# Layer 0's node table in rows of 268 values, x read from the input: a two-layer graph attention kernel

## The chip, the cores and the metric

The kernel runs on one core of a Trainium2 chip. The metric is the device time of one execution in microseconds, the median of several runs. The core has five engines that run their own instruction streams and signal each other: TensorE (PE), VectorE (DVE), ScalarE (ACT), GpSimd (POOL) and SyncE (SP); 16 DMA engines move data between DRAM and the on-chip memory (SBUF).

## The reference

A graph of N = 6250 nodes with 256 features each and E = 200000 edges, sorted by destination, with 32 attributes each. Two layers of graph attention with 4 heads and then 1:

```python
def _gat(x, src, dst, ea, Wg, a_s, a_d, Wge, a_e, b, n, h, f):
    hx = (x @ Wg).reshape(n, h, f)
    he = (ea @ Wge).reshape(-1, h, f)
    al = leaky_relu(einsum('nhf,hf->nh', hx, a_s)[src] + einsum('nhf,hf->nh', hx, a_d)[dst]
                    + einsum('ehf,hf->eh', he, a_e), 0.2)
    m = segment_max(al, dst, num_segments=n)
    al = exp(al - m[dst])
    al = al / segment_sum(al, dst, num_segments=n)[dst]
    out = segment_sum(hx[src] * al[:, :, None], dst, num_segments=n)
    return out.reshape(n, h * f) + b

h = maximum(layernorm(x), 0)
# in each layer: te = relu(edge_attr @ We + be) * exp(h @ Wo + bo)[src]; a loop edge per node
# with the mean te of its edges; layer 0: h1 = relu(_gat(h, ...) + h); layer 1: h2 = _gat(h1, ...) + h1
# result: x + h2 + h
```

## The kernel before, in words

**Tables.** For each layer there is a table in DRAM, `T[l]`, with one row per node. The useful part of a row of layer 0 has `TW` = 268 float32 values: the 256 projected features, 4 logit parts of the source, the gate exp(h Wo + bo), a one, 4 logit parts of the destination, and the two numbers (scale and offset) of the layer norm. A row of layer 1 has 260. Each row is stored twice as wide: its second half holds the node's own features, x for layer 0, the layer's input for layer 1. So the table is read in two ways: as N rows of 2 TW values, when the nodes of a step are loaded with their x, and as 2N rows of TW values, when rows are gathered by source (`self.rows`). The source indices `self.src` (128 partitions, one column per chunk of 128 edges) are therefore doubled.

**The start** (`prologue`, L203) makes the layer-0 table. The nodes are cut into 49 tiles of 128, in nine groups of 2, 5, 7, 7, 7, 7, 7, 5 and 2; after them come 24 tiles whose rows of x are gathered directly (`first_rows`, L252) for the first step's edges. A loop over the tiles writes out by hand which part of which tile comes next on each engine: statistics (DVE), `norm` (ACT, L318), `turn` (two transposes on PE, L324, copied by ACT, L326), `mult` (PE, L452), `keep` (DVE adds the bias into one of three `trow` buffers, L456), and for each group `store` (L339), which sends its rows to the table by an SP DMA (L343). `keep_x` (L346) copies a group's x into the second halves from the input `xt`, DRAM to DRAM, by an SP DMA (L350); one is issued every fourth tile from tile 8 on. `xt` is x padded with zeros to 268 values a row. Among the tiles, one piece at a time, `indices` (L458) prepares the index tables on DVE: it loads `sc0`, `bcol`, `drow`, `r4`, `src` and `dpv` by SP DMAs in this order, doubles `src` in four DVE operations (L478), and then works on the others (L481 and on).

**The steps** (`edges`, L649). Each layer is 66 steps of up to 24 chunks of 128 edges; a step covers the edges of at most 112 destination nodes. The pieces of a step are interleaved by the order of calls in the loop. Around the change:

- `nodes` (L905) issues one SP DMA for a step two ahead: 112 rows `tw` (the row and x) at a row number that SP loads into a register.
- `gather` (L839) issues the 24 indirect DMAs of the next step on POOL (L846): each fetches 128 rows by 128 indices of `src`. Three buffers `G` take turns.
- `logits` makes the edge logits on DVE, closing with two scans (L1058, L1060). `ends` (L1064) then has PE transpose their last columns (L1067).
- `spread` (L952, DVE L964 and L965, the wide operation L964 once for two steps), `parts` (DVE L993 to L996, PE L1001), `rphase1` and `rphase2` (the edge features on PE and ACT) belong to the next step; `links` (DVE L1077, L1079, PE L1084), `maxima` and `scale` (DVE L1148, 6.3 us) to this one.
- `sums` (PE L1160) adds the scaled rows by destination, 48 matmuls into one bank `u`; `evict` (ACT L1165) copies it to `U`. `finish`, one step later, makes the nodes' result; in layer 0 `rows3` stores it to `T[1]` by an SP DMA (L1294).

`ending` (L744) does the last two steps of a layer. A second program for other graphs (`general`, L1307) is built but not run with these inputs.

Of the kernel before, what the change touches and what calls it, by code (L numbers as in the profile page):

```python
# [22 lines left out]
F32 = mybir.dt.float32  # L23
BF = mybir.dt.bfloat16
I32 = mybir.dt.int32
AF = mybir.ActivationFunctionType
OP = mybir.AluOpType
# [4 lines left out]
P = 128  # L32
C = 24
SE = P * C
NX = 24
D = 256
# [3 lines left out]
M = 112  # L40
# [39 lines left out]
class Kernel:  # L80
# [10 lines left out]
    def run(self):  # L91
        nc, tc = self.nc, self.tc
        self.cp = self.pool("consts")
        self.dp = self.pool("tables", space=DRAM)
        N = self.N
        self.T = [self.dp.tile([N + P, L.TW * 2], F32, name=f"T{L.l}") for L in self.L]

        self.rows = [t[0:N + P, :].rearrange("n (k w) -> (n k) w", w=L.TW) for t, L in zip(self.T, self.L)]
        with ExitStack() as c:
            c.enter_context(tc.manual_schedule())  # L100
            self.gp = [self.pool("gath0", 1, c)]
            self.ps_k = self.pool("ps_k", 1, c, space=PSUM)
            self.lp = self.pool("loads", 2, c)
            self.offs = offs = np.concatenate([[0], np.cumsum(self.cs)]).tolist()
            self.steps = [dict(L=L, s=s, C=self.cs[s], o=offs[s], k=L.l * self.NS + s)
                          for L in self.L for s in range(self.NS)]
            self.prologue()
            self.edges(c)
        self.general()
# [93 lines left out]
    def prologue(self):  # L203
        nc, tc, cp, a, N = self.nc, self.tc, self.cp, self.a, self.N
        L = self.L[0]
        H = L.H
        NT = -(-N // P)
        GT = 7
        CX = self.CX = min(self.cs[0], NX)
        V = nc.vector  # L210
        with ExitStack() as c:
            xp = self.pool("x", 1, c)
            wp = self.pool("pw", 2, c)
            pt = self.pool("pt", 2, c, space=PSUM)
            starts = sorted({*range(0, NT, GT), min(2, NT), max(NT - 2, 0)} - {NT})
            groups = [list(range(g, e)) for g, e in zip(starts, starts[1:] + [NT]) if g < e]
            g0 = len(groups)
# [25 lines left out]
            zero = wp.tile([P, 2 * L.TW], F32, name="zero", bufs=1)  # L243
            nc.gpsimd.memset(zero, 0.0)
            if NT * P < N + P:
                nc.sync.dma_start(self.T[0][NT * P:N + P, :], zero[:N + P - NT * P, :2 * L.TW])
            trows = [wp.tile([P, GT, L.TW], F32, name=f"trow{i}", bufs=1) for i in range(3)]
            ln = wp.tile([P, NT + CX, 2], F32, name="ln", bufs=1)

# [89 lines left out]
            def store(g):  # L339
                n, ts, trow = len(groups[g]), groups[g], trows[g % 3]  # L340
                nc.scalar.activation(trow[:, :n, L.ln:L.ln + 2], ln[:, ts[0]:ts[0] + n, :], AF.Copy)
                nc.scalar.activation(trow[:, :n, L.g:L.g + 1], trow[:, :n, L.g:L.g + 1], AF.Exp)
                nc.sync.dma_start(self.T[0][0:NT * P, :].rearrange("(p t) d -> p t d", p=P)  # L343
                                  [:, ts[0]:ts[0] + n, 0:L.TW], trow[:, :n, :])

            def keep_x(g):  # L346
                ts, n = groups[g], len(groups[g])
                to, of = (t.rearrange("(p t) d -> p t d", p=P)[:, ts[0]:ts[0] + n, :]
                          for t in (self.T[0][0:NT * P, L.TW:2 * L.TW], a["xt"][0:NT * P, :]))
                nc.sync.dma_start(to, of)  # L350

            lead = stats(0)
            for _ in range(6):
# [17 lines left out]
            for k in range(-3, len(tiles) + 1):  # L371
                if k == 6:
                    next(index)
                    gi = self.index_load(0, wp)
                    index = chain(index, self.index_group(0, wp, gi))
                if k > 10 and k % 2 or k > NT:
                    next(index, None)
                n0 = next(tail, None) if k >= NT // 2 else None
                if n0 is not None:
                    w = min(P, N + P - n0)  # L380
                    nc.sync.dma_start(self.T[1][n0:n0 + w, :], zero[:w, :2 * self.L[1].TW])
                if k == 5:
                    more()
                if k >= 8 and k % 4 == 0 and k // 4 - 2 < g0:
                    keep_x(k // 4 - 2)
                if 0 <= k + 1 < len(tiles):
                    turn(*tiles[k + 1])
                if 0 <= k + 3 < len(tiles):
                    g, i, t = tiles[k + 3]
                    if i == 0:  # L390
                        load(g + 3)
                        drain(ahead.pop(g, ()))
                    norm(g, i, t)
                step(g + 2)
                if t >= NT:
                    step(g + 2)
                if 0 <= k - 1 < len(tiles):
                    keep(*tiles[k - 1])
                step(g + 2)
                if t >= NT:  # L400
                    step(g + 2)
                if 0 <= k < 10 or k >= 14 and k % 4 == 0:
                    next(rows0, None)
                if k >= NT + 2:
                    next(later, None)
                if k == max(NT - 6, 7):
                    while not hasattr(self, "flags"):
                        next(index)
                    next(index)
                    self.load_lb(0)  # L410
                    self.load_ea(0)
                    self.load_fl(0)
                if 0 <= k < len(tiles):
                    mult(*tiles[k])
                while kept < g0 and groups[kept][-1] <= k - (3 if k < NT - 3 else 1):
                    store(kept)
                    kept += 1
# [40 lines left out]
    def indices(self, wp):  # L458


        nc, cp, a = self.nc, self.cp, self.a
        NS, NCH, N = self.NS, self.NCH, self.N
        V = nc.vector
# [9 lines left out]
        dpv = wp.tile([P, NS], I32, name="dpv", bufs=1)  # L473
        nc.sync.dma_start(dpv, a["dpv"])
        yield
        for i in range(0, NCH, 392):
            src = self.src[:, i:min(NCH, i + 392)]
            V.tensor_scalar(src, src, 2.0, None, op0=OP.mult)  # L478
            yield
        scf = wp.tile([P, 11, NS], F32, name="scf", bufs=1)  # L480
        V.tensor_copy(scf, sc0)  # L481
        V.memset(scf[:, 0, 0:1], 0.0)
# [20 lines left out]
        for r in range(2):  # L503
            n = (NS + 1 - r) // 2
# [334 lines left out]
    def gather(self, st):  # L839
        nc, L = self.nc, st["L"]  # L840
        st["G"] = G = self.G0 if st["k"] == 0 else self.gp[st["k"] % 3].tile([P, C, 270], F32, name="G")
        n = self.N
        idx = self.src[:, st["o"]:st["o"] + st["C"]]
        last = st["C"] - 1
        for c in (range(0) if st["k"] == 0 and self.CX > last else (last, *range(last))):
            nc.gpsimd.indirect_dma_start(  # L846
                out=G[:, c, 0:L.TW], out_offset=None, in_=self.rows[L.l][0:2 * n, :],
                in_offset=bass.IndirectOffsetOnAxis(ap=idx[:, c:c + 1], axis=0))

    def pair(self, k):  # L850
# [54 lines left out]
    def nodes(self, st):  # L905
        nc, L, s = self.nc, st["L"], st["s"]
        st["r"] = r = self.row(0, s)
        tw = self.tws[st["k"] % 4]
        st["tw"], st["xw"] = tw[:, :L.TW], tw[:, L.TW:L.TW + D]
        w = L.TW + D  # L910
        nc.sync.dma_start(tw[1:M + 1, :w], self.T[L.l][ds(r, M), 0:w])

    def halves(self, st):

# [147 lines left out]
        yield  # L1062

    def ends(self, st):  # L1064

        e = st["ends"]
        self.nc.tensor.transpose(self.lf[0:e.shape[1], 1:P + 1], e, self.ident)  # L1067
# [255 lines left out]
    def general_layer(self, L, wp, pp):  # L1323
        nc, tc, N, a = self.nc, self.tc, self.N, self.a
        V = nc.vector
        l, H = L.l, L.H
# [10 lines left out]
        with tc.For_i(0, self.NCH * P, P) as i:  # L1337
            si = wp.tile([P, 1], I32, name="gsi")
            di = wp.tile([P, 1], I32, name="gdi")
# [7 lines left out]
            G = wp.tile([P, 272], F32, name="gG")  # L1347
            nd = wp.tile([P, L.TW], F32, name=f"gnd{l}")
            old = wp.tile([P, L.W], F32, name=f"gold{l}")
            sw, dw = [wp.tile([P, 1], I32, name=n) for n in ("gsi2", "gdi2")]  # L1350
            V.tensor_scalar(sw, si, 2.0, None, op0=OP.mult)
            V.tensor_scalar(dw, di, 2.0, None, op0=OP.mult)
            for t, tab, ix in ((G[:, :L.TW], self.rows[l], sw), (nd, self.rows[l], dw), (old, state, di)):
                nc.gpsimd.indirect_dma_start(out=t, out_offset=None, in_=tab[:, :],
                                             in_offset=bass.IndirectOffsetOnAxis(ap=ix[:, 0:1], axis=0))
# [19 lines left out]
            t = wp.tile([P, P], F32, name="gt")  # L1375
# [11 lines left out]
            for v, f in ((G, G[:, L.p:L.p + H]), (old, e[:, 1, :H])):  # L1387
# [8 lines left out]
                                         out_offset=bass.IndirectOffsetOnAxis(ap=di[:, 0:1], axis=0))  # L1396
# [26 lines left out]
def drain(g):  # L1423
    for _ in g:
        pass
# [22 lines left out]
def layout(inputs):  # L1448
    x = np.ascontiguousarray(inputs["x"])
    src, dst, ea = (np.asarray(inputs[k]) for k in ("src", "dst", "edge_attr_32"))  # L1450
    N, E = x.shape[0], src.shape[0]
    cs = cuts(E)
    NS, NCH = len(cs), sum(cs)
    a = {"x": np.concatenate([x, np.zeros((2 * P, D), np.float32)])}
    a["xt"] = np.concatenate([a["x"], np.zeros((N + 2 * P, Layer(0).TW - D), np.float32)], 1)
    EP = NCH * P
    gdst = np.full(EP, N, np.int32)
    gdst[:E] = dst
# [13 lines left out]
    o = 0  # L1472
# [22 lines left out]
    for l, H in enumerate(HEADS):  # L1495
        w = {n: np.asarray(inputs[f"L0_gnn_{n}{l}"]) for n in _W}
# [23 lines left out]
```

## Time and profile before

| | us |
|---|---|
| median of 3 runs | 4721.76 |
| lowest, highest | 4721.40, 4724.88 |
| the profiled execution | 4717.79 |
| its span in the profile | 4716.0 |

| engine | busy us | share of the span |
|---|---|---|
| PE | 3204.3 | 68% |
| DVE | 2842.0 | 60% |
| ACT | 524.2 | 11% |
| POOL | 3015.5 | 64% |

The mean granted clock of PE is 0.73. The first gather from the layer-0 table starts at 105.6 us, the steps of layer 0 fill the time up to some 2370 us, those of layer 1 the rest. A line of the timeline gives start, duration, engine, line of the kernel, operation, result `<-` operands, the count of instructions taken together, and in brackets how long the engine stood before it and what it stood for. "SPq" is a DMA issued by SyncE, "PEld" TensorE's loading of weights. A line of the groups gives the same for all instructions of one kind: busy time and mean in ns, then the idle time before them, with what ended most of it. A line of the waits gives who waited `<-` for whom: total us, times, longest us.

### The profile page before, as it was taken

The numbers are of one execution on the slowest core, as the hardware profiler recorded it, in microseconds if no ns is written. First come the engines' busy times: TensorE is split into PE (matmuls) and PEld (weight loads), VectorE is DVE, ScalarE is ACT, GpSimd is POOL, SyncE is SP. The second block draws the span as 40 slices with busy tenths as digits, with TensorE's granted clock in tenths as the row PEclk, the third lists the DMA queues.
The fourth block names the chain that finished last, engine by engine and source line by source line (L and its number), as shares of the span: only waits on it lengthen the run. The fifth ranks groups of instructions, "written<-read, shape, count | busy, mean of one in ns | idle before, by whom it ended". The sixth has DMA issues, their size and how long they took to land. (4 is left out here: it accounts for less than half of the span.)

```text
span 4716.0 us, 33666 instructions
## 1 busy us (share of the span) xinstructions
PE 3204.3 (68%) x9878; PEld 1931.3 (41%) x9878; DVE 2842.0 (60%) x6122; ACT 524.2 (11%) x1162; POOL 3015.5 (64%) x3255
## 2 busy tenths in 40 slices
PE   7677677776777777777755666666666666666666
PEld 5344444444444444444433334343433333343434
DVE  6566676666676666666664555555545555554546
ACT  4111111111111111111110000000000000000000
POOL 5566666666666666666636666666666666666664
PEclk8767767767777777676676777776777777776777
DMA  8344444444444444444434444444444444444442
GB/s 275 94 128 128 117 126 131 119 127 128 116 127 129 125 122 126 127 121 126 122 84 113 120 118 127 116 123 121 124 117 122 127 121 119 119 125 114 122 124 74
DMA packets 234171, 582.99 MB, mean 124 GB/s; under 512 B 62185, under 2 KB 84613, under 8 KB 233913
## 3 DMA queue, kind: packets, MB, share of 16 engines
q0 software_dynamic: 150144, 422.75, 34.1%
q1 hardware_dynamic: 83419, 157.36, 10.1%
q8 instruction: 79, 1.29, 0.1%
q14 instruction: 113, 0.93, 0.1%
q10 hardware_dynamic: 416, 0.67, 0.1%
HBM read 549.44 MB, written 37.92 MB: 125 GB/s over the span
## 5 line engine op out<-in xcount | busy, mean ns | idle before, releaser
L846 POOL DMA_INDIRECT G<-T,src x3102 | 2962.0, 955 | 1623.1 <-issue 898.9
L1160 PE MATMUL u<-G,S 128*128 128x270 f32 (+1 forms) x6252 | 1621.4, 411 | 750.2 <-issue 628.7
L1160 PEld LDWEIGHTS u<-G,S 128*128 128x128 f32 x6252 | 1235.8, 200 | 1075.8 <-issue 682.0
L935 PE MATMUL y<-ea,webd 64*128 64x384 f32 (+1 forms) x1056 | 734.8, 822 | 304.5 <-issue 269.2
L1148 DVE TENSOR_TENSOR G<-G,kps 128x6144 f32<-128x6144 f32 (+3 forms) x136 | 853.0, 6275 | 0.0
L1077 DVE TENSOR_TENSOR_SCAN cl<-fl,cl,lf 4x129 f32<-4x129 f32 (+1 forms) x130 | 61.2, 471 | 937.2 <-remote 657.0
L935 PEld LDWEIGHTS y<-ea,webd 64*128 64x128 f32 x1056 | 290.2, 298 | 597.1 <-issue 534.7
L949 PE MATMUL zad<-R,wea 128*64 128x384 f32 (+1 forms) x1056 | 464.3, 794 | 2.3 <-ACT R L940 1.0
L980 DVE TENSOR_TENSOR S<-kps,loc 128x3072 f32<-128x3072 f32 x132 | 437.6, 3315 | 4.5
L940 ACT ACTIVATE R<-y,webd 128x768 f32<-128x768 f32 x260 | 233.1, 897 | 627.6 <-PE y L935 272.3
L949 PEld LDWEIGHTS zad<-R,wea 128*64 128x64 f32 x1056 | 155.9, 202 | 314.1 <-issue 253.5
L1165 ACT ACTIVATE U<-u 128x270 f32<-128x270 f32 (+1 forms) x132 | 51.9, 393 | 1880.4 <-remote 913.1
L1029 DVE STREAM_TRANSPOSE rt<-zad 128x768 f32<-128x768 f32 (+1 forms) x130 | 124.5, 958 | 35.2 <-remote 27.8
L1067 PE MATMUL lf<-ident,fb 128*36 128x128 f32 (+1 forms) x132 | 47.1, 357 | 138.2 <-issue 108.7
L1001 PE MATMUL zad<-a,Q 128*128 128x12 bf16 (+1 forms) x132 | 24.4, 185 | 156.6 <-issue 98.5
L452 PE MATMUL fin<-wg,h1T 128*128 128x260 f32 x264 | 127.2, 632 | 1.8 <-ACT h1T L1255 1.8
L1094 DVE TENSOR_TENSOR fb<-flpen,lf 128x192 f32<-128x192 bf16 (+1 forms) x132 | 36.7, 278 | 148.2 <-PE lf L1084 128.6
L964 DVE TENSOR_TENSOR lb<-lb,kps 128x1536 bf16<-128x1536 bf16 (+1 forms) x68 | 113.0, 1661 | 0.0
L452 PE MATMUL ps<-wg,hT 128*128 128x266 f32 x292 | 89.9, 436 | 33.3 <-ACT hT L326 14.9
L452 PEld LDWEIGHTS fin<-wg,h1T 128*128 128x128 f32 x264 | 71.5, 299 | 48.5 <-issue 34.6
L1001 PEld LDWEIGHTS <-Q 128*128 128x128 bf16 x132 | 14.9, 113 | 180.2 <-issue 104.4
L1190 ACT ACTIVATE mw<-mw,mg 128x2 f32<-128x2 f32 x66 | 19.7, 298 | 608.0 <-DVE mg L1189 337.1
(191 smaller groups left out, 2079.4 us busy)
## 6 DMA issues: line engine op xcount, KB each, us to landing
G<-T,src POOLq DMA_INDIRECT x3102
ea<-in_ea_dram SPq DMA_DIRECT2D x64, 768.0 KB
lb<-locrow SPq DMA_DIRECT2D x64, 384.0 KB
tw<-T SPq DMA_DIRECT2D x66, 229.2 KB
T<-t1row SPq DMA_DIRECT2D x66, 227.5 KB
tw<-T SPq DMA_DIRECT2D x66, 225.8 KB
out_dram<-fb SPq DMA_DIRECT2D x64, 112.0 KB
T<-in_xt_dram SPq DMA_DIRECT2D x5, 938.0 KB
```

What stands on the lines that cost most here:

```text
L452: self.nc.tensor.matmul(ps[:, :L.MW], hT[:, k, :], self.wg[L.l][:, k, :], start=(k == 0), stop=(k == 1))
L846: nc.gpsimd.indirect_dma_start(out=G[:, c, 0:L.TW], out_offset=None, in_=self.rows[L.l][0:2 * n, :], in_offset=bass.IndirectOffsetOnAxis(a ...
L935: nc.tensor.matmul(y[:, o], self.webd[l][r, :], ea[r, w], start=True, stop=True)
L940: nc.scalar.activation(R[:, i, :32 * c].rearrange("p (b n) -> p b n", b=2), y.rearrange("p (b n) -> p b n", b=2)[:, :, :16 * c], AF.Relu, ...
L949: nc.tensor.matmul(st["zad"][i * PH:(i + 1) * PH, o], self.wea[l][0], R[:, i, w], start=True, stop=False)
L964: V.tensor_tensor(lb[:, :, :n], lb[:, :, :n], self.k_part.unsqueeze(2).to_broadcast([P, i, n]), op=OP.is_equal)
L980: nc.vector.tensor_tensor(st["S"][:, c0:c1, :], self.k_iota.unsqueeze(1).to_broadcast(w), self.loc[:, o + c0:o + c1].unsqueeze(2).to_broad ...
L1029: V.transpose(rv[:, :32 * c].rearrange("p (b n) -> p b n", b=2), z.rearrange("p (b n) -> p b n", b=2)[:, :, :16 * c])
L1077: V.tensor_tensor_scan(cl[:H, :], fl[:H, :], lf[:H, 0:P + 1], init, op0=OP.add, op1=OP.max)
L1148: nc.vector.tensor_tensor(v, v, pw[:, c0:c1, :].unsqueeze(3) .to_broadcast([P, c1 - c0, H, L.F]), op=OP.mult)
L1160: nc.tensor.matmul(st["u"][:, :L.W], S[:, i, :], G[:, i, 0:L.W], start=(j == 0), stop=(j == c - 1))
L1165: self.nc.scalar.activation(U[:, :L.W], st["u"][:, :L.W], AF.Copy)
```

## The change

The layer-0 table gets rows of 268 values, without x. With that

- `keep_x` and the input `xt` go; a store of rows writes 7 x 268 contiguous values per partition where it wrote 268 of every 536;
- `nodes` loads, in layer 0, the 112 rows of 268 from the table and the 112 rows of x from the input `x`, in two SP DMAs into the same tile;
- layer 0 gathers with the source numbers as they are. Layer 1, whose rows stay double, needs them doubled: a DVE operation in `ends` of each layer-0 step doubles the columns of that step, 128 x 24 integers;
- the program for other graphs follows.

Each engine's own order beside that: on DVE the index work that stood behind the doubling comes some eight places earlier, and the new operation of a step stands between the scan L1060 and, where there is one, the spread L964; it has no wait of its own. On SP nine DMAs go and 66 come, with their register instructions. PE, ACT and POOL have the same instructions in the same order.

```diff
-        self.T = [self.dp.tile([N + P, L.TW * 2], F32, name=f"T{L.l}") for L in self.L]
+        self.T = [self.dp.tile([N + P, L.TW * (1 + L.l)], F32, name=f"T{L.l}") for L in self.L]
...
-                nc.sync.dma_start(self.T[0][NT * P:N + P, :], zero[:N + P - NT * P, :2 * L.TW])
+                nc.sync.dma_start(self.T[0][NT * P:N + P, :], zero[:N + P - NT * P, :L.TW])
...
-                nc.sync.dma_start(self.T[0][0:NT * P, :].rearrange("(p t) d -> p t d", p=P)
-                                  [:, ts[0]:ts[0] + n, 0:L.TW], trow[:, :n, :])
-
-            def keep_x(g):
-                ts, n = groups[g], len(groups[g])
-                to, of = (t.rearrange("(p t) d -> p t d", p=P)[:, ts[0]:ts[0] + n, :]
-                          for t in (self.T[0][0:NT * P, L.TW:2 * L.TW], a["xt"][0:NT * P, :]))
-                nc.sync.dma_start(to, of)
+                nc.sync.dma_start(self.T[0][0:NT * P, :].rearrange("(p t) d -> p t d", p=P)[:, ts[0]:ts[0] + n, :],
+                                  trow[:, :n, :])
...
-                if k >= 8 and k % 4 == 0 and k // 4 - 2 < g0:
-                    keep_x(k // 4 - 2)
...
-        for i in range(0, NCH, 392):
-            src = self.src[:, i:min(NCH, i + 392)]
-            V.tensor_scalar(src, src, 2.0, None, op0=OP.mult)
-            yield
...
-                out=G[:, c, 0:L.TW], out_offset=None, in_=self.rows[L.l][0:2 * n, :],
+                out=G[:, c, 0:L.TW], out_offset=None, in_=self.rows[L.l][0:n * (1 + L.l), :],
...
-        w = L.TW + D
+        w = L.TW + L.l * D
         nc.sync.dma_start(tw[1:M + 1, :w], self.T[L.l][ds(r, M), 0:w])
+        if L.l == 0:
+            nc.sync.dma_start(st["xw"][1:M + 1, :], self.a["x"][ds(r, M), :])
...
     def ends(self, st):
 
+        if st["L"].l == 0:
+            src = self.src[:, st["o"]:st["o"] + st["C"]]
+            self.nc.vector.tensor_scalar(src, src, 2.0, None, op0=OP.mult)
+
         e = st["ends"]
         self.nc.tensor.transpose(self.lf[0:e.shape[1], 1:P + 1], e, self.ident)
...
-    a["xt"] = np.concatenate([a["x"], np.zeros((N + 2 * P, Layer(0).TW - D), np.float32)], 1)
```

More of the change, by code (lines that the diff above doesn't have):

```diff
@@ L1349, in general_layer @@
             old = wp.tile([P, L.W], F32, name=f"gold{l}")
-            sw, dw = [wp.tile([P, 1], I32, name=n) for n in ("gsi2", "gdi2")]
-            V.tensor_scalar(sw, si, 2.0, None, op0=OP.mult)
-            V.tensor_scalar(dw, di, 2.0, None, op0=OP.mult)
+            sw, dw = [wp.tile([P, 1], I32, name=n) for n in ("gsi2", "gdi2")] if l else (si, di)
+            if l:
+                V.tensor_scalar(sw, si, 2.0, None, op0=OP.mult)
+                V.tensor_scalar(dw, di, 2.0, None, op0=OP.mult)
             for t, tab, ix in ((G[:, :L.TW], self.rows[l], sw), (nd, self.rows[l], dw), (old, state, di)):
```

## The prediction

> **What bounds the kernel now.** I read the profile's page first (groups of instructions), then the busy time by windows, then the timeline of single steps of each layer and of the start. All sums are made against the profiled execution: span 4716.0 us, 4717.79 us on the clock of the runs; the median of the runs shown is 4721.76, 4.0 us above it, so I add 4.0 at the end. From the page:
>
> ```profile
> L846 POOL DMA_INDIRECT G<-T,src x3102 | 2962.0, 955 | 1623.1 <-issue 898.9
> ...
> L964 DVE TENSOR_TENSOR lb<-lb,kps 128x1536 bf16<-128x1536 bf16 (+1 forms) x68 | 113.0, 1661 | 0.0
> ```
>
> The same group of gathers, in the windows 190 to 2350 us (steps of layer 0) and 2560 to 4600 us (steps of layer 1):
>
> ```profile
> L846 POOL DMA_INDIRECT G<-T,src x1468 | 1408.7, 960 | 759.1 <-issue 422.6 <-PE u L1160 269.4 <-PE fin L1253 24.1
> L846 POOL DMA_INDIRECT G<-T,src x1430 | 1359.4, 951 | 681.3 <-issue 416.3 <-remote 200.7 <-PE y L935 30.6
> ```
>
> A gather takes 0.955 us and is followed by some 0.30 us of "issue", so the 24 of a step cost about 30 us. 1468/24 = 61.2 steps in 2160 us are 35.3 us a step in layer 0; 1430/24 = 59.6 in 2040 us are 34.2 in layer 1. The rest of a step is the pause between groups. The timeline of layer 1 shows what it is made of:
>
> ```profile
> 2897.41 10.80 PE L1160 MATMUL u<-G,S 128*128 128x261 f32 x43
> ...
> 2903.12 0.33 SPq L911 DMA_DIRECT2D tw<-T  x1
> ...
> 2914.96 0.95 POOL L846 DMA_INDIRECT G<-T,src  x1 [0.30 <-issue]
> ...
> 2920.13 0.39 ACT L1165 ACTIVATE U<-u 128x261 f32<-128x261 f32 x1 [18.79 <-remote]
> ...
> 2920.37 0.95 POOL L846 DMA_INDIRECT G<-T,src  x1 [4.46 <-remote]
> ```
>
> The sums in PE were over at 2908.2, yet ACT's eviction of them began only at 2920.13, 4.2 us after the group's last gather (2915.91). I call this **the hold**: from a few us after the node load (tw) on, signals between engines arrive late, and all come at once about 4.2 us after the last gather. So a step of layer 1 is 30 + 4.2. Layer 0 has the same floor, and on top of it sums that are not done when the hold begins:
>
> ```profile
> 1018.60 10.07 PE L1160 MATMUL u<-G,S 128*128 128x270 f32 x43 [1.57 <-DVE crow L1136]
> ...
> 1028.13 0.34 SPq L911 DMA_DIRECT2D tw<-T  x1
> ...
> 1031.54 0.39 PE L1160 MATMUL u<-G,S 128*128 128x270 f32 x1 [1.74 <-issue]
> ...
> 1034.70 0.95 POOL L846 DMA_INDIRECT G<-T,src  x1 [0.30 <-issue]
> ...
> 1039.58 0.40 ACT L1165 ACTIVATE U<-u 128x270 f32<-128x270 f32 x1 [11.47 <-PE u L1160]
> ...
> 1039.81 0.95 POOL L846 DMA_INDIRECT G<-T,src  x1 [4.17 <-PE u L1160]
> ...
> 1040.18 0.33 DVE L1060 TENSOR_TENSOR_SCAN fb<-pen,al 128x96 f32<-128x96 bf16 x1
> ...
> 1040.43 1.73 DVE L964 TENSOR_TENSOR lb<-lb,kps 128x1536 bf16<-128x1536 bf16 x1
> ...
> 1043.02 0.17 DVE L996 TENSOR_TENSOR a<-a3r,a 128x8 bf16<-128x8 f32 x1
> ...
> 1043.25 0.19 PE L1001 MATMUL zad<-a,Q 128*128 128x12 bf16 x1 [2.29 <-DVE a L996]
> ```
>
> 43 sums run at 0.23 us each before the hold; inside it one comes about every 2 us (0.39 of work behind 1.74 of nothing). Whatever delays the sums in layer 0 can lengthen the pause.
>
> The other part is the start, 0 to 152 us:
>
> ```profile
> 0.00:60.00 60.00, 42.81 (x166) 29.38 (x167) 39.28 (x169) 24.63 (x61) 33.45 (x94) 0.89 0.90 288
> 60.00:105.00 45.00, 39.66 (x196) 32.00 (x195) 37.11 (x172) 29.08 (x79) 17.94 (x57) 0.92 0.94 285
> ```
>
> (Columns: PE, PEld, DVE, ACT, POOL, granted clock, DMA share, GB/s.) And from the timeline of that stretch:
>
> ```profile
> 41.83 3.94 SPq L350 DMA_DIRECT2D T<-in_xt_dram  x2
> 45.19 0.36 DVE L478 TENSOR_SCALAR src<-src 128x392 int32<-128x392 int32 x1 [11.14 <-DMA src<-in_src_dram]
> ...
> 46.37 2.11 PE L452 MATMUL ps<-wg,hT 128*128 128x266 f32 x4 [6.86 <-DVE trow L456]
> ...
> 92.68 0.43 DVE L456 TENSOR_TENSOR trow<-ps,bias 128x266 f32<-128x266 f32 x1 [2.50 <-DMA T<-trow]
> ...
> 94.34 2.65 SPq L343 DMA_DIRECT2D T<-trow  x3
> ...
> 104.89 2.15 SPq L911 DMA_DIRECT2D tw<-T  x3
> ...
> 105.61 0.94 POOL L846 DMA_INDIRECT G<-T,src  x1 [22.34 <-ACT hT L326]
> ...
> 138.73 0.39 ACT L326 ACTIVATE hT<-pT 128x256 f32<-128x256 f32 x1 [11.02 <-remote]
> ...
> 151.01 0.43 DVE L456 TENSOR_TENSOR G<-ps,bias 128x266 f32<-128x266 f32 x1 [0.46 <-PE ps L452]
> ...
> 152.07 0.94 POOL L846 DMA_INDIRECT G<-T,src  x1 [16.75 <-ACT pen L927]
> ```
>
> The DMA engines are 90 to 94% busy. DVE stands 11.14 us for the load of src, which is in the doubling's way, and PE 6.86 us of it. The last three row stores are issued from 94.3 to 97.0, and the node loads and first table gathers follow their landing at 104.9 and 105.6, 8 us later. A hold lies over this group too, and step 0's tiles, half done when it began, end at 151.
>
> **The change, part by part.**
>
> *The copy of x goes* (nine DMAs, L346):
>
> ```profile
> T<-in_xt_dram SPq DMA_DIRECT2D x5, 938.0 KB
> T<-in_xt_dram SPq DMA_DIRECT2D x2, 670.0 KB
> T<-in_xt_dram SPq DMA_DIRECT2D x2, 268.0 KB
> ```
>
> That is 6.6 MB, at the 288 GB/s of the windows 23 us of all DMA engines in a stretch where they are the scarce thing. The stores of rows, as large, stay; each partition's part becomes one run of 7504 bytes for seven tiles. I don't count 23 us, because compute does not run on the DMAs alone: PE is busy 88% of the 45 us from 60 on. I count what stalls show: the 2.50 us before L456 at 92.68 and the 8 us that the last row stores take to land, of which I take half: 2.5 + 4 = 6.5.
>
> *The doubling leaves the start.* Four DVE operations of 0.35 us go, and with them the 11.14 us wait; PE's share of it, 6.86, is the gain. What is late next is the following index work, which reads smaller loads issued ahead of src; it moves forward by eight places, and its latest load could hold DVE for up to some 4 us of the 6.86. So −7, at worst −3.
>
> Together −13.5 at the first gather. It is followed by its own 30 us and the hold; what the tiles of step 0 lose by an earlier hold they did not gain before it, so I carry −13 to the end of the start (bounds: −8 if the store lands as late as now; −17 if the stretch behaves as DMA-bound).
>
> *Doubling in the loop*, 66 DVE operations on 128x24 integers. No trace shows that size; the nearest rows:
>
> ```profile
> L1179 DVE TENSOR_SCALAR cnt<-U x66: 132/134/136, 215.1 to 2430.0; 128x1 f32<-128x1 f32 x66
> L621 DVE TENSOR_SCALAR loc<-gt x18: 177/210/435, 99.1 to 2391.1; 128x96 bf16<-128x96 f32 x16, 128x14 bf16<-128x14 f32 x1, 128x13 bf16<-128x13 f32 x1
> ```
>
> So 0.13 to 0.21 us; nearer to the first, I take 0.17. The operation waits for nothing new: it stands behind the scan L1060, and the gather that reads these indices was over in the step before. What is queued behind it is the spread (L964) in every second step, and the parts that PE waits for; in the other steps DVE waits for PE there. The waits in 190 to 2350 us tell the two apart:
>
> ```profile
> PE zad L1001 <- DVE a L996: 38.2, 18, 2.5
> DVE cl L1077 <- PE zad L1001: 75.3, 38, 5.8
> ```
>
> With spread (68 such operations on the page, 34 a layer) PE stands 2.29 us for DVE at 1043.25, and there 0.17 us goes straight to the scale and the sums. Without it DVE waits for PE (38 of 62 steps) and covers it: nothing. 33 × 0.17 = 5.6 us, if each delay passes on once; 0 if the hold's floor hides it; 66 × 0.21 = 14 if nothing covers it. I take +6.
>
> *x by its own load.* Each layer-0 step issues one more SP DMA of 112 x 1024 bytes, while tw shrinks from 112 x 2096 to 112 x 1072. The issue costs SP about 0.34 us (the row at 1028.13) and its registers; behind it queue the loads for steps ahead. tw is asked for two steps ahead, and no wait for it shows in layer 0; steps of layer 1 have other extra loads in every second step and keep their 34.2 us. Price 0; if the cover fails, 0.34 × 66 = 22, rival E. The Trainium skill ("DMA: Bandwidth & Descriptors", Rules for kernel authors) says to coalesce many small transfers into one large, which speaks against this part; its Anatomy section puts the fixed part of a DMA at about 2.0 us, by which the split would add, by estimate, 132 us if nothing overlapped it. The same rules say that an early issue overlaps that cost; with loads two steps ahead the trace sides with this.
>
> *Narrow rows under the gathers.* Their cadence is POOL's (0.955 + 0.30) and the two layers differ little with rows of 1072 and 1040 bytes: 0.
>
> Sum: −13 + 6 = −7; 4717.8 − 7 = 4710.8, and on the scale of the median (4721.8) **4714.8**.
>
> **Rivals.**
>
> *A: the loop pays nothing.* The operation falls into DVE's idle time in all steps (many of its waits of 1 to 2.5 us lie inside the hold), and the start gains 13 to 17. For it: the step that ends at 1039.81 sits on the floor (4.17). Against: the PE wait on L996. Time 4721.8 − 15 = 4707.
>
> *B: the start's gain is lost.* DVE stops at a later index load, and the earlier hold catches step 0 with more tiles undone. For it: the group of 30 us and the hold remain, 11.02 us of ACT's waiting at 138.73. Against: what the hold delays is work that would otherwise have come before it, so it moves with the rest. Gain 4, cost 6: 4724.
>
> *C: slower, by the sums slipping into the hold.* Place: steps with spread, and any other whose sums start late. Price: 0.17 us more ahead of the scale pushes one more sum over the hold's onset, where it takes about 2 us instead of 0.23, and leaves 0.4 us or so behind the hold's end; 62 × 0.4 = 25 us. It decides once a layer-0 step grows by more than 13/62 = 0.21 us. For it: the row at 1031.54 and the 1.1 us by which layer 0 exceeds layer 1. Against: some steps already have their sums done at the floor. Time 4721.8 − 13 + 25 = 4734.
>
> *D: the gathers themselves get faster* from the packed table, against a cadence that shows no data limit. If it took the 1.1 us between the layers from a third of the 62 steps, −23 beside the forecast's −7: 4692.
>
> *E: the split load is not covered.* Were SP late with the loads behind x's, or x late for its reader, each layer-0 step would pay one more issue: 22 us beside the forecast's −7, 4737. For it: SP blocks 3.94 us on two copies at 41.83. Against: that is the DMA-bound start. The Trainium skill's rule on coalescing, above, speaks for it.
>
> **How the numbers follow.** A difference of 0.2% (9.4 us: 4712.3 to 4731.2) is about what a measurement of this kernel tells from no change. Forecast (start −10 to −16, loop 0 to +10): chance 0.54, own range 4706 to 4722, of which 0.22 lies below 4712.3 and 0.32 within. A: 0.15, faster. B: 0.08, same. C: 0.16, slower. D: 0.04, faster. E: 0.03, slower. Faster 0.41, same 0.40, slower 0.19. The range takes in A and B whole and C at its price, not E or D: 4700 to 4735.
>
> **What would show it.** In the new profile: no DVE idle on src near 34 to 45 us, PE's 6.86 us gone, and the first table gather near 92 instead of 105.6; the second group near 139 instead of 152. The mean step of layer 0 should grow by about 0.1 us, the new operation should read 0.13 to 0.21 us, and layer 1 should stay at 34.2. A first gather later than 98 would refute the start's gain; a layer-0 step longer by over 0.2 us would be C; a shorter one A or D; a tw or x wait on DVE or ACT would mean that the split load is not covered.

## The result, and the profile after

| | before | changed |
|---|---|---|
| median of 22 runs each, us | 4722.68 | 4715.79 |
| lowest, highest | 4719.44, 4727.24 | 4706.96, 4721.23 |
| the profiled execution's span | 4716.0 | 4711.8 |

The ratio is 0.9985, 95% interval [0.9979, 0.9992]: 6.9 us less (3.8 to 9.9), where the forecast was 4714.8. It is under the 0.2% that a few runs would tell; with 22 runs its sign is clear.

The experiments ran on several chips, and these were of two kinds, which the prediction did not know of: where the result was taken the hold is there, on others it is missing and the same kernel before takes some 4087 us. Each experiment is compared with the kernel before on its own chip.

Where the time went shows in the start and in the steps of layer 0. First the start of the changed kernel, by the timeline:

```profile
36.34 0.54 DVE L469 CAST scf<-sc 128x726 f32<-128x726 int32 x1 [0.68 <-DMA sc<-in_sdst_dram]
...
45.02 0.60 DVE L488 TENSOR_SCALAR lrow<-drow,bcf 66x768 bf16<-66x768 int32 x1
...
75.47 8.82 SPq L343 DMA_DIRECT2D T<-trow  x3
...
88.54 0.36 SPq L899 DMA_DIRECT2D tw<-T  x1
89.11 0.34 SPq L901 DMA_DIRECT2D tw<-in_x_dram  x1
...
89.27 0.94 POOL L834 DMA_INDIRECT G<-T,src  x1 [14.29 <-DMA T<-trow]
...
121.16 0.38 ACT L326 ACTIVATE hT<-pT 128x256 f32<-128x256 f32 x1 [11.04 <-remote]
...
139.00 0.44 DVE L448 TENSOR_TENSOR G<-ps,bias 128x266 f32<-128x266 f32 x1 [0.46 <-PE ps L444]
...
140.06 0.94 POOL L834 DMA_INDIRECT G<-T,src  x1 [21.10 <-ACT pen L917]
```

DVE's 11.14 us before the doubling are gone; the first piece of index work waits 0.68 us. The last row store is issued by 84.3 us instead of 97.0 and lands in 4.3 us instead of 7.9 (to the first node load, at 88.54 and 104.89), and the first table gather starts at 89.27 instead of 105.61. The windows of the start show DMA let off from 60 us on (its share is the column before the last):

```profile
0.00:60.00 60.00, 50.39 (x211) 35.97 (x211) 47.47 (x203) 31.40 (x79) 39.50 (x116) 0.91 0.86 286
60.00:105.00 45.00, 34.98 (x167) 27.73 (x165) 30.13 (x142) 23.97 (x63) 23.69 (x49) 0.91 0.68 195
```

In the first 60 us PE did 50.4 us of work where it had done 42.8. Of the 16.3 us by which the first gather is earlier, 12.0 are left at the second group (152.07 to 140.06). The hold comes earlier too and finds fewer of step 0's tiles done: behind its end (121.16) they take until 139.0, 18 us, where they took 12 (138.73 to 151.01).

Then the groups of gathers in 190 to 2350 and in 2560 to 4600 us:

```profile
L834 POOL DMA_INDIRECT G<-T,src x1465 | 1405.5, 959 | 755.1 <-issue 423.9 <-PE u L1154 262.2 <-PE fin L1247 38.6
L834 POOL DMA_INDIRECT G<-T,src x1430 | 1360.2, 951 | 680.8 <-issue 415.7 <-remote 213.6 <-PE y L925 30.5
```

Layer 1 is as before (x1430 in both). For layer 0 I take from the trace the starts of the groups, from the third on, over 62 steps: 2176.5 us before (193.1 to 2369.6), 2184.1 changed (180.9 to 2365.0). So the start wins 12.2 and the steps of layer 0 lose 7.6; the spans differ by 4.2. These are two single executions, and that of the kernel before was a fast one: 4717.79 us, below all of its 22 runs, while the changed kernel's, 4714.12, is 1.7 below its median. If the start's 12.2 holds for the medians, the loop lost some 5 us, an estimate from 12.2 and 6.9. The new operation, by its line in 190 to 2350 us:

```profile
L1058 DVE TENSOR_SCALAR src<-src x61: 145/152/388, 217.3 to 2340.2; 128x24 int32<-128x24 int32 x61
```

All this is close to the forecast's −13 and +6. Whether it came about for the reasons given is what the experiments ask.

### The profile page after: what moved, and what is told of

Read it like the earlier page. It is cut to its first block, busy times and chain, and to the rows that moved or that the text cites. A ratio compares the mean times of both kernels' runs of the same rounds, so it can differ in the third digit from the quotient of the medians.

```text
span 4711.8 us, 34013 instructions
## 1 busy us (share of the span) xinstructions
PE 3213.4 (68%) x9878; PEld 1937.4 (41%) x9878; DVE 2847.5 (60%) x6184; ACT 524.5 (11%) x1162; POOL 3015.4 (64%) x3255
## 5 line engine op out<-in xcount | busy, mean ns | idle before, releaser
L1154 PE MATMUL u<-G,S 128*128 128x270 f32 (+1 forms) x6252 | 1642.4, 415 | 744.0 <-issue 630.4
L1154 PEld LDWEIGHTS u<-G,S 128*128 128x128 f32 x6252 | 1249.0, 202 | 1081.4 <-issue 679.7
```

Of the source, the lines that this page charges most:

```text
L1154: nc.tensor.matmul(st["u"][:, :L.W], S[:, i, :], G[:, i, 0:L.W], start=(j == 0), stop=(j == c - 1))
```

## The experiments

**The start: the wait on src put back, the copy put back, and the doubling moved.** All three with the split load alone on one chip, one without the hold, where the kernel before took 4085.82 us.

`e1_wait_back`, to the changed kernel, at the doubling's old place:

```diff
+        for i in range(0, NCH, 392):
+            src = self.src[:, i:min(NCH, i + 392)]
+            V.tensor_scalar(src, src, 1.0, None, op0=OP.mult)
+            yield
```

> The changed kernel with four DVE operations of src times 1 put back at the place where the doubling stood in the start, so that DVE waits there for the load of src again; the loop keeps its doubling. My theory (the removed wait on src is about half of the start's gain): DVE idle of some 9 to 12 us before the first of them, the first table gather moves from 89.3 to about 96 us, the second group from 140.1 to about 146, and the time is 5 to 7 us above the changed kernel, about 4721. Rival (the copy of x alone made the gain, DVE's wait was slack of PE's buffers): the second group stays within 2 us of 140 and the time within 2 us of the changed kernel, about 4716.

`e2_copy_back`, to the changed kernel:

```diff
+        self.spare = self.dp.tile([N + P, 2 * self.L[0].TW], F32, name="spare")
...
+            def keep_x(g):
...
+                          for t in (self.spare[0:NT * P, L.TW:2 * L.TW], a["xt"][0:NT * P, :]))
+                nc.sync.dma_start(to, of)
...
+                if k >= 8 and k % 4 == 0 and k // 4 - 2 < g0:
+                    keep_x(k // 4 - 2)
```

The input `xt` is back with it; the rows of the table stay packed.

> The changed kernel with the nine DRAM to DRAM copies put back at their places in the start, into a spare table with rows of the same pitch that nothing reads. My theory (copy traffic delays the row stores' landing and blocks their buffers): the first table gather moves from 89.3 to about 96 us, the second group from 140.1 to about 146, total about 4721. Rival (only the wait on src counted): the second group stays within 2 us of 140, total about 4716. A third reading, that both hide behind the same stretch, would have this run and the one with the wait put back each lose far less than half of the 12 us that the second group gained, or one of them nearly all.

`e3_double_later`, to the kernel before: the loop of L476 to L479 stands behind the flag stores (L524), all four operations in one piece.

> The kernel before with its four doubling operations moved behind the flag stores in the start's index work, where src has long landed; table, copies and node loads as before. My theory: DVE's 11 us wait goes, PE's 6.9 us with it, and the second group moves from 152.1 to about 146, total about 4716 against 4722.7. Rival (the start is bound by DMA until the copies go, so the wait was slack): second group within 2 us of 152, total about 4722.

`e6_split_only`, to the kernel before:

```diff
-        w = L.TW + D
+        w = L.TW + L.l * D
         nc.sync.dma_start(tw[1:M + 1, :w], self.T[L.l][ds(r, M), 0:w])
+        if L.l == 0:
+            nc.sync.dma_start(st["xw"][1:M + 1, :], self.a["x"][ds(r, M), :])
```

> The kernel before in which only the node load of layer 0 is split in two (268 values of the row from the table, x from the input); copy, doubling and wide table stay. My theory (the second load is hidden by being two steps ahead): mean layer-0 step 35.1 us within 0.05, total 4722.7 within 3 us. Rival (the split load costs the loop its 8 us, not the new DVE operation): mean layer-0 step 35.2 or more, total about 4730. If x's load shifts the onset of the hold, the step changes by more than 0.1 us in either direction.

Measured, beside the changed kernel itself, which ran on two other chips without the hold (on the last of them the split load ran once more, as `e9_split_again`):

| kernel | median, us | ratio to before, interval | first table gather | third group |
|---|---|---|---|---|
| e6_split_only (start as before) | 4085.86 | 0.9999 [0.9990, 1.0009] | 107.00 | 167.06 |
| e3_double_later | 4087.51 | 1.0004 [0.9995, 1.0014] | 106.28 | 166.36 |
| e2_copy_back | 4079.24 | 0.9984 [0.9975, 0.9993] | 101.36 | 163.44 |
| e1_wait_back | 4080.92 | 0.9987 [0.9978, 0.9996] | 97.31 | 163.75 |
| e9_split_again (start as before) | 4083.47 | 1.0000 [0.9991, 1.0009] | 106.41 | 166.45 |
| e4_changed_again | 4079.12 | 0.9971 [0.9960, 0.9983] | 88.82 | 157.72 |
| e11_changed_last | 4074.64 | 0.9975 [0.9966, 0.9984] | 88.47 | 157.37 |

Two rows of the table, and the profiled kernel before (105.61), have the same start; their first gathers differ by 1.4 us, so a smaller difference says nothing. The waits of the start say more. First `e6_split_only`, then `e3_double_later` (0 to 152 us), then `e1_wait_back` (0 to 170):

```profile
DVE src L478 <- DMA src<-in_src_dram: 13.2, 1, 13.2
...
DVE st L273 <- DMA x<-in_x_dram: 6.1, 2, 4.5
```

```profile
DVE st L273 <- DMA x<-in_x_dram: 12.6, 4, 4.6
...
DVE scf L477 <- DMA sc<-in_sdst_dram: 3.0, 1, 3.0
```

```profile
DVE src L470 <- DMA src<-in_src_dram: 12.5, 1, 12.5
...
DVE st L273 <- DMA x<-in_x_dram: 1.6, 1, 1.6
```

With the copies in place, taking the wait away gains 0.7 us at the first gather (107.00 to 106.28), which is nothing that these runs can tell from no gain, and 1.0004 in time: DVE gets past the doubling's place and then stands for the next loads, 12.6 us for x instead of 6.1 and 3.0 for the first index table. Without the copies the same wait costs 8.5 (97.31 against 88.82). Putting the copies back costs 12.5 (101.36). The parts are not terms of a sum: the wait counts only once the DMA engines are free enough (in the first 60 us their share is 0.91 in `e3_double_later` and 0.74 in `e1_wait_back`). There is a third part that the prediction has at nothing. `e2_copy_back` and `e3_double_later` both have the copies and no wait, yet the first gather is at 101.36 in the one and 106.28 in the other; the one has the packed rows and no doubling in the start, the other wide rows and four operations of 0.35 us. Which of the two makes these 4.9 us no run separates.

So the rival of `e3_double_later` was right, and my theory of it wrong. At the first gather the theory's shifts for the other two came, 8.5 and 12.5 where about 7 was expected. In time `e1_wait_back` and `e2_copy_back` keep 4.9 and 6.6 us of a gain that is 9.8 to 11.6 with both away. The third group, which on such a chip is the first that waits for step 0's work, moves less than the first gather (9.1 of 17.9 us, `e9_split_again` to `e11_changed_last`, on one chip):

```profile
88.47 0.94 POOL L834 DMA_INDIRECT G<-T,src  x1 [14.30 <-DMA T<-trow]
...
157.37 0.94 POOL L834 DMA_INDIRECT G<-T,src  x1 [8.96 <-ACT pen L917]
```

These rows are of `e11_changed_last`. From there to the end of layer 0 POOL never stands 1 us, so the total follows the third group: −9.8 us there, −11.6 for `e4_changed_again` on its own chip.

> The changed kernel itself, so that the others of this call have it on their own chip. The last call's chip showed no hold: gathers ran on without the 4 us pause and the kernel before took 4085.8 us. On such a chip my theory expects only the start's gain and nothing lost in the loop: with the wait back 4080.9 and with the copy back 4079.2, the changed kernel should come to 4070 to 4076. Rival (the third group of gathers waits for step 0's work, which all of these reach at about 163 us, whatever the first gather does): 4078 to 4081. On a chip with the hold: 4716 against 4722.7.

4079.12 lies in the rival's 4078 to 4081, but only because this chip is slower: the kernel before took 4090.76 there, 4.9 us more than on the chip that the ranges were made for. Against its own chip the changed kernel gained 11.6, where the theory stands for 10 to 16 and the rival for 5 to 8, and its third group starts at 157.72 us, not at the rival's 163. So the theory held, and again with `e11_changed_last`.

**The loop: the operation doubled, moved away, and taken nine times.** `e5_op_twice`, to the changed kernel, with a spare tile that is set to zero once ahead of the steps:

```diff
             self.nc.vector.tensor_scalar(src, src, 2.0, None, op0=OP.mult)
+            self.nc.vector.tensor_scalar(self.spare, self.spare, 1.0, None, op0=OP.mult)
```

> The changed kernel with a second DVE operation of the same kind and size (on a spare tile) behind the doubling in each step of layer 0. On a chip with the hold my theory (the operation lies on the path in steps with spread) expects 5 to 8 us over the changed kernel and a layer-0 step longer by some 0.1 us; the rival (the loop's loss comes from the split load or from a shifted pattern of steps) none. On a chip without the hold POOL has no pause to lengthen and both expect the changed kernel's time within 1 us.

`e6_double_at_end`, to the changed kernel: the operation leaves `ends`, and `ending` gets, in front of the first gather of layer 1,

```diff
         if after:
+            for i in range(0, self.NCH, 392):
+                src = self.src[:, i:min(self.NCH, i + 392)]
+                nc.vector.tensor_scalar(src, src, 2.0, None, op0=OP.mult)
             self.gather(after)
```

> The changed kernel without the operation in the loop: src is doubled by four DVE operations of 128x392 after layer 0's last results, where POOL waits for the last rows of layer 1's table to land. On a chip with the hold my theory expects the loop's loss back: layer-0 step 35.1 instead of 35.2, total 5 to 8 us under the changed kernel, about 4709. Rival (split load or chance): the changed kernel's time within 2 us. On a chip without the hold: no difference from the changed kernel, or up to 1.4 us more if the four operations of 0.35 us lie in front of the first gather of layer 1.

Their chip had no hold: 4077.13 us, ratio 0.9968 [0.9956, 0.9980], and 4078.02, ratio 0.9971 [0.9960, 0.9983], beside the changed kernel's 0.9971. There the operation has no price, once, twice or not at all; for the question itself these two runs are inconclusive. A second run of the kernel with the operation moved away, and one with eight further operations (`range(8)` around the line added above), had a chip with the hold, where the kernel before took 4718.79:

> The changed kernel with eight further DVE operations of the same kind and size (on a spare tile) behind the doubling in each step of layer 0: some 8 x 0.15 = 1.2 us more of DVE per step, 80 us in all. On a chip with the hold my theory (in steps with spread DVE's time passes to the sums and so to the pause) expects the layer-0 step longer by 0.5 to 1.2 us and the time 30 to 80 us over the changed kernel; the rival (DVE's time is covered, the loop's loss of some 5 us has another cause) under 10 us. On a chip without the hold POOL's gathers set the step as long as the rest of a step fits in their 30 us: the changed kernel's time within 3 us by my theory, and 80 us more only if DVE had no slack there.

> The changed kernel with the doubling at the end of layer 0 instead of in the loop, once more. On a chip with the hold my theory expects the loop's loss of about 5 us back: ratio to the kernel before about 0.9973 where the changed kernel had 0.9985; rival: 0.9985. On a chip without the hold both expect the 0.9971 that the changed kernel and this one had in the last call.

Measured: `e7_op_eight` 4750.72, ratio 1.0062 [1.0048, 1.0076]; `e8_end_again` 4714.17, ratio 0.9994 [0.9985, 1.0003]. The theory's 0.9973 for the latter is outside its interval; the rival's 0.9985 is at its edge. The gathers in 190 to 2350 us, of `e7_op_eight` and then of `e8_end_again`:

```profile
L836 POOL DMA_INDIRECT G<-T,src x1446 | 1384.7, 958 | 775.5 <-issue 417.0 <-PE fin L1251 162.7 <-PE u L1158 117.4
```

```profile
L837 POOL DMA_INDIRECT G<-T,src x1464 | 1403.5, 959 | 757.2 <-issue 421.9 <-PE u L1153 233.0 <-PE fin L1246 57.7
```

Over the same 62 steps: 2217.2 us with eight more operations, 2184.1 changed, 2187.3 with the operation moved away, 2176.5 before. The changed kernel and the one before were traced on the chip of the result, where the kernel before takes 3.9 us more than here, so a few us between the pairs mean little. What DVE spends does reach the step: `e7_op_eight` is 33.1 us longer, at the lower end of the theory's 30 to 80. Its spare operations in 190 to 2350 us:

```profile
L1062 DVE TENSOR_SCALAR spare<-spare 128x24 int32<-128x24 int32 x480 | 90.7, 189 | 74.3 <-remote 44.5 <-DVE spare L1062 16.8
```

They are 90.7 us of work in 60 steps, 1.51 a step, 2.75 with the idle time between them. Where they land shows when the steps are taken apart by kind. In all four traces every second step is one with spread. There PE waits for the parts that stand behind the operation on DVE, in the changed kernel and then in `e7_op_eight`, which has two rows of it (190 to 2350 us):

```profile
PE zad L991 <- DVE a L986: 39.6, 22, 2.5
```

```profile
PE zad L993 <- DVE a L988: 76.6, 21, 4.6
...
PE zad L993 <- DVE a L987: 38.1, 9, 4.5
```

Of the 61 steps with 24 gathers, the 31 with spread grew by 39.0 us, 1.26 each; the 30 others became 6.3 shorter. In the steps with spread the first sum starts 17.3 us after the group instead of 14.9, and 7.9 sums instead of 4.3 run later than 3 us behind the last gather. So the path that the prediction names is there, and it ends as rival C has it, with sums left behind the hold.

Over all steps the growth is 33.1/62 = 0.53, a share of 0.2 to 0.35 of what the operations took. If one operation of 0.152 us passes on by the same share, it costs 0.03 to 0.05 us a step, 2 to 3 us in all, an estimate. And the kernel without any operation in the loop has not won the loop's loss back; its 62 steps are 3 us longer than the changed kernel's. So the operation explains a part of the loss at most.

**The split load.** With that the second load became the suspect:

> The kernel before with only the node load of layer 0 split in two, once more, for a chip with the hold. Moving the doubling out of the loop did not bring the loop's 5 us back there, so the first theory (the single operation costs them) is in doubt. Theory 2 (the second load, or its registers on SP, costs them): mean layer-0 step about 35.2 instead of 35.1 and the time 4 to 8 us over the kernel before. Theory 3 (the layer-0 step varies by about 0.1 us with any shift of the pattern, and no part has a price of its own): within 4 us of the kernel before, either sign. On a chip without the hold: the kernel before's time, as in the first call.

`e10_four_more`, to the changed kernel, with a spare tile of 128x256:

```diff
             nc.sync.dma_start(st["xw"][1:M + 1, :], self.a["x"][ds(r, M), :])
+            for i in range(4):
+                nc.sync.dma_start(self.spare[28 * i:28 * i + 28, :], self.a["x"][ds(r, 28), :])
```

> The changed kernel with four further SP loads per layer-0 step, 28 rows of x each, into a spare tile: the split's price five times over, at little data. Theory 2 (each extra load costs a layer-0 step 0.1 us): step longer by some 0.4 us, time 20 to 30 us over the changed kernel. Theory 3 (SP's loads are covered two steps ahead): the changed kernel's time within 5 us. On a chip without the hold both expect the changed kernel's time within 2 us, unless SP itself becomes late.

> The changed kernel itself beside the two others of this call. On a chip with the hold: ratio 0.9985 to the kernel before as in the result; on a chip without it 0.9971 as in the second call.

Their chip had no hold either (before: 4084.44 us). `e9_split_again`: 4083.47, ratio 1.0000 [0.9991, 1.0009]. `e10_four_more`: 4075.53, ratio 0.9978 [0.9968, 0.9987], beside 0.9975 of `e11_changed_last`. There the split, once or with four more loads, costs nothing that can be measured. With the hold it was not run by itself, and the rest of the loop's loss stays without a shown cause.

## Why the prediction was right, point by point

**The sum** was −7 and came out at −6.9 (3.8 to 9.9). Its two terms were about right as sums over a stretch. The mechanism of the first held in the main, with parts of other sizes; that of the second exists, but was sized twice too large, and the loss came near its figure by luck.

**The start, −13: measured −12.0 at the second group.** The half of the last stores' landing that I took, 4 us, came (7.9 to 4.3). The stalls, 2.5 for the copy and 7 for the wait on src, were too little: the last store goes out 12.7 us earlier. And they can't be priced one by one. The copies are worth 9.7 together with the packed rows when they go first (107.00 to 97.31), 12.5 alone when they go last; the wait next to nothing when it goes first, 8.5 when it goes last. I read DVE's 11.14 us and PE's 6.86 as gains of their own, although the windows that I quoted gave the DMA engines as 90% busy; the idle time moves to the next load as long as that holds. The packed rows I had at nothing ("the stores of rows, as large, stay"); up to 4.9 us of the first gather may be theirs. Then "what the hold delays moves with the rest" was too simple, and rival B had something right: the first gather gained 16.3, more than my 13.5, and 4.3 of it were given back as the earlier hold left 18 us of tiles behind it instead of 12.

**The doubling in the loop, +6: a loss of 7.6 was there, the operation explains 2 to 3 of it.** The operation's length was right (0.152 us in a range of 0.13 to 0.21), and so was the place: `e7_op_eight` lengthens the steps with spread and no others. What was wrong is the size. I let the delay pass on whole in all 33 such steps, while the row that I quoted has PE waiting for the parts in 18 of 62; 18 × 0.152 is 2.7, close to what `e7_op_eight` gives. I also left out that the steps in between take some of it back (0.21 us each there). `e8_end_again` shows a loss with no operation in the loop at all. What the rest is, no run here tells. Step by step the 61 full steps of the changed kernel differ from those before with a standard deviation of 0.78 us, either way, which over 61 steps makes 6 us without any part having a price: a shift of the pattern is enough for 7.6, and so may be the split load inside the hold, which was not run. That the two executions gave a figure near +6 was luck.

**x by its own load, 0:** right where it could be measured, on chips without the hold (ratios 0.9999 and 1.0000), where POOL has no pause that a late signal could lengthen. Of the 132 us that the prediction has from the Trainium skill's Anatomy section nothing shows there; the section gives its 2.0 us for DMAs that GpSimd issues, and these are issued by SyncE. The Trainium skill's rule against many small transfers ("DMA: Bandwidth & Descriptors", Rules for kernel authors) has no price there either: four more loads of 28 rows per step moved the ratio from 0.9975 to 0.9978. Inside the hold one thing shows, in the issues of x's load in 190 to 2350 us:

```profile
L901 SPq MOVE tw<-in_x_dram x61: 5/697/1384, 208.2 to 2331.1; - x61
L901 SPq DMA_DIRECT2D tw<-in_x_dram x61: 317/698/1347, 209.0 to 2331.8; - x61
```

The issue took 0.70 us instead of the 0.33 of tw, and so did the register move ahead of it (0.03 for tw); both fall into the hold. No engine waits for tw or x in that stretch of the trace.

**The hold** was read rightly in its length and its end, but not in its beginning. I put it "a few us after the node load". A step of the changed kernel, whose group began at 998.29:

```profile
1011.44 9.92 PE L1154 MATMUL u<-G,S 128*128 128x270 f32 x42 [0.40 <-issue]
...
1019.51 0.34 SPq L899 DMA_DIRECT2D tw<-T  x1
1021.56 0.39 PE L1154 MATMUL u<-G,S 128*128 128x270 f32 x1 [0.20 <-issue]
...
1024.33 0.71 SPq L901 DMA_DIRECT2D tw<-in_x_dram  x1
1024.36 0.39 PE L1154 MATMUL u<-G,S 128*128 128x270 f32 x1 [2.42 <-issue]
```

The node load no longer waits for the readers of x and is issued, in the mean over 61 steps of the trace, 22.1 us after the group's start instead of 24.8. The first slow sum (the first one, from 15 us after the group's start on, that PE stood over 1 us before) comes 25.7 us after the start in both. So the hold does not follow that load; what starts it is open.

**The gathers' cadence** is unchanged (955 ns in both), so rival D falls, and E where it could be measured. Rival C's price is not seen at one operation; `e7_op_eight` shows that its mechanism exists: 3.6 more sums behind the hold in a step with spread, which grows by 1.26 us.

## What to carry to other kernels

A stall that ends with a DMA can be worth nothing by itself while the DMA engines are full: here the same wait of VectorE, 11 to 13 us long, was worth next to nothing with the copies in place and 8.5 us without them, so price such edits together and in both orders. When the steps of a loop vary by more than the effect that is sought, a mean step that moves as forecast confirms nothing; put the cost away altogether and take it many times over, see whether both move, and take the steps apart by kind, since a mean over all of them hid here that one kind paid and the other did not. Compare each run with the kernel before on its own chip, never with a figure in microseconds from another. And a time that comes out right may do so for a wrong reason: the term to trust is the one whose removal was run.

## What the runs showed of the hardware that was not expected

The hold does not belong to the kernel. Where one kernel of a chip showed it all did, and where one lacked it none had it; no chip of the experiments was used at two times, so whether it belongs to the chip or to the time is open. On three chips no pause stands between the groups, and the same program is 13% shorter: 4085.82, 4090.76 and 4084.44 us for the kernel before, against 4722.68 and 4718.79. The gathers of all layers on the page of `e4_changed_again`, and of the changed kernel on a chip with the hold:

```profile
L834 POOL DMA_INDIRECT G<-T,src x3102 | 2959.9, 954 | 1009.0 <-issue 913.7
```

```profile
L834 POOL DMA_INDIRECT G<-T,src x3102 | 2962.2, 955 | 1627.5 <-issue 900.2
```

A gather takes the same time on both; POOL's idle time is 618 us less without the hold. On a chip without it no part of this change inside the loop had a price that shows, and only the start is worth something.
